# Second expert layer of each tile issued between the two halves of the next tile's first layer

## The chip, the cores and the metric

The kernel runs on one core of one Trainium2 chip. A core has five engines that run their own instruction streams and wait for each other by semaphores: TensorE (PE, matrix products, with its weight loads shown as PEld), VectorE (DVE), ScalarE (ACT), GpSimd (POOL) and SyncE (SP, which here only issues transfers). Each engine has a sequencer that reads its instructions in order and hands them on; the sequencer itself executes waits, branches, register arithmetic and loads of a register from memory. The metric is the device time of one launch in microseconds (us), lower is better. Before the change the median of three runs is 1127.79 us (1126.37 to 1128.49).

## The reference

1250 tokens of 1024 numbers in fp32. A two-layer graph convolution over 40,000 edges comes first, then a mixture of experts. The part that matters here is the second one:

```python
t = layernorm(x)                                   # 1250 x 1024
logits = silu(t @ rw1 + rb1) @ rw2 + rb2           # 8 experts
w = softmax over the 2 largest logits of each token, 0 elsewhere
eh = silu(einsum('td,edh->teh', t, ew1) + eb1)     # 1024 -> 256 hidden, per expert
eo = einsum('teh,ehd->ted', eh, ew2) + eb2         # 256 -> 1024, per expert
out = x + t + einsum('te,ted->td', w, eo)
```

Every token needs two of the eight experts only.

## The kernel before, in words

The graph layers and the router run first and are not touched. For the experts the kernel sorts the 2500 pairs of token and expert into tiles of 128 slots, each tile belonging to one expert, which is known only at run time. 23 tiles (0 to 22) are worked on in this execution. All expert weights lie in one on-chip buffer `xw`; which part a product reads is an address worked out from the tile's expert number, loaded into a register (`values_load`, L1511) by PE's and ACT's sequencers.

The steps of one tile, by the names of the code:

- `gather(i)` (L1492, POOL): an indirect DMA brings the tile's 128 token rows into one of three buffers.
- `spread_bias(i)` (L1487, SP): a DMA spreads the expert's output bias over 128 partitions into one of four buffers `ybs`.
- `fetch(i)` (L1503, L1506): eight PE transposes into PSUM and two ACT copies give the tokens transposed, `xT`.
- `first_layer(i)` (L1511, L1520, L1526): PE's and ACT's sequencers load the expert number; then eight matrix products of 128x128 by 128x256 accumulate in one PSUM buffer `ps`. Each is two instructions in the trace (fp32), so x16. A DVE copy (L1526; ACT for tile 0) takes the result into `hx`.
- `turn_hidden(i)` (L1533, L1535): two PE transposes of `hx` and two ACT activations (SiLU) give the hidden values transposed, `hT`.
- `second_layer(i)` (L1542, L1547, L1552, L1553): ACT scales the bias by the slot weight; four products (x8 in the trace) fill two PSUM buffers of 512 columns; two DVE instructions (L1552) weight the result and add the bias into `yo`, one of two buffers; POOL issues an indirect DMA that adds the 128 rows to the output (the scatter). All scatters add to the same tensor, so each waits until the one before it has landed.

`section` runs the tiles as a pipeline. In the step of tile i it issues, in this order: the gather for tile i + 3, the bias and `fetch` of tile i + 1, `turn_hidden` of tile i - 1, then `first_layer(i)` and `second_layer(i - 1)`. The order on PE and ACT is that of the code (a manual schedule); on DVE, POOL and SP a scheduler sets it when the program is built. `first_layer` takes an optional function `middle`, called between its fourth and fifth product. Tiles 1 and 3 use it for parts of the plan of the remaining tiles (`slots`, `slot_weights`), tile 0 too.

Tiles 0 to 19 always run. Behind them come branches on the number of tiles (`sections`, L1599): tiles 20 to 22 form the section that runs here, with tile 19's second half of the work joined to it. `end_of_last` then does `turn_hidden` and `second_layer` of tile 22 alone. In that section's last step (tile 22), where no `fetch` is due, `second_layer(21)` already stands in the middle of `first_layer(22)`: `early` is set there and nowhere else.

Of the kernel before, what the change touches and what calls it, by code (L numbers as in the profile page):

```python
# [29 lines left out]
def kernel(  # L30
# [967 lines left out]
    def moe():  # L998
# [383 lines left out]
        def slot_weights(at_tile, nb, i0, i1, take):  # L1382
            n = i1 - i0
            at_w = take([P, 2 * nb, 3, n], BF)
            at_w = at_w.rearrange("p (c b) i t -> p c b i t", c=2)
            for i in range(3):
                tt(
                    at_w[:, :, :, i, :], at_tile,
                    w_parts[i][:, :, :nb, None].to_broadcast([P, 2, nb, n]), ALU.mult,
                )  # L1390
            pw = by_slot(lambda c, b: at_w[:, c, b].rearrange("p i t -> p (i t)"), nb, 3 * n)
            nc.vector.tensor_reduce(
                w_slot[:, i0:i1], pw.rearrange("p (i t) -> p t i", t=n), AX.X, ALU.add
            )
# [87 lines left out]
        def spread_bias(i):  # L1482
            e = nc.values_load(
                eid[0:1, i : i + 1], engines=(ENG.SP,), min_val=0, max_val=E - 1,
                skip_runtime_bounds_check_because="eid is a count of experts, cut at E - 1",
            )
            nc.sync.dma_start(  # L1487
                out=ybs[i % 4], in_=eb2[ds(e, 1), :].partition_broadcast(P)
            )

        def gather(i):
            nc.gpsimd.indirect_dma_start(  # L1492
                out=xgs[i % 3], out_offset=None, in_=t_d[:N, :],
                in_offset=bass.IndirectOffsetOnAxis(ap=ids[:, i : i + 1], axis=0),
            )

        def fetch(i):
            xg = xgs[i % 3]
            xT = xTb[i % 2]
            for q in range(0, KD, 4):  # L1500
                pt = tpp.tile([P, 4, P], F32, name="tp")
                for k in range(4):
                    nc.tensor.transpose(  # L1503
                        pt[:, k, :], xg[:, (q + k) * P : (q + k + 1) * P], ident
                    )
                nc.scalar.copy(xT[:, q : q + 4, :], pt)  # L1506
            return xT

        def first_layer(i, xT, middle=None):

            e = nc.values_load(  # L1511
                eid[0:1, i : i + 1], engines=(ENG.PE, ENG.Activation),
                min_val=0, max_val=E - 1,
                skip_runtime_bounds_check_because="eid is a count of experts, cut at E - 1",
            )
            ps = mm.tile([P, 512], F32, name="ps")
            for k in range(KD):
                if k == KD // 2 and middle is not None:
                    middle()
                nc.tensor.matmul(  # L1520
                    ps[:, :H], xT[:, k, :], w1_all[:, ds(e, 1), k * H : (k + 1) * H],
                    start=(k == 0), stop=(k == KD - 1),
                )
            hx = hxs[i % 2]

            (nc.scalar.copy if i == 0 else nc.vector.tensor_copy)(hx, ps[:, :H])  # L1526
            return e, hx

        def turn_hidden(i, e, hx):
            pt = mm.tile([P, 512], F32, name="ps").rearrange("p (q n) -> p q n", n=P)  # L1530
            hT = hTs[i % 2]
            for q in range(KH):
                nc.tensor.transpose(pt[:, q, :], hx[:, q * P : (q + 1) * P], ident)  # L1533
            for q in range(KH):
                nc.scalar.activation(  # L1535
                    hT[:, q, :], pt[:, q, :], AF.Silu, bias=eb1_p[:, ds(e, 1), q : q + 1]
                )
            return e, hT

        def second_layer(i, e, hT):  # L1540
            yo, yb = yos[i % 2], ybs[i % 4]
            nc.scalar.activation(yb, yb, AF.Copy, scale=w_slot[:, i : i + 1])  # L1542
            for h in range(2):
                dc = slice(h * HALF, (h + 1) * HALF)
                ps = mm2.tile([P, 512], F32, name="ps2")
                for q in range(KH):
                    nc.tensor.matmul(  # L1547
                        ps, hT[:, q, :],
                        w2_all[:, ds(e, 1), q * D + h * HALF : q * D + (h + 1) * HALF],
                        start=(q == 0), stop=(q == KH - 1),  # L1550
                    )
                stt(yo[:, dc], ps, w_slot[:, i : i + 1], yb[:, dc], op0=ALU.mult, op1=ALU.add)  # L1552
            nc.gpsimd.indirect_dma_start(  # L1553
                out=out[:, :],
                out_offset=bass.IndirectOffsetOnAxis(ap=to[:, i : i + 1], axis=0),
                in_=yo, in_offset=None, bounds_check=N - 1, oob_is_err=False,
                compute_op=ALU.add,
            )
# [6 lines left out]
        xTs, held = {}, {}  # L1565

        def section(i0, i1, joined=True, until=None, middle=None):

            for i in range(i0, i1):
                if i + 3 < NTILE and i > 1:  # L1570
                    gather(i + 3)
                ahead = i + 1 < (until or i1)
                if ahead:
                    spread_bias(i + 1)
                    xTs[i + 1] = fetch(i + 1)
                rest = None
                if i > i0 or joined:
                    turned = turn_hidden(i - 1, *held.pop(i - 1))
                    rest = lambda: second_layer(i - 1, *turned)

                early = rest if not ahead and until is None else None
                held[i] = first_layer(i, xTs.pop(i), middle or early)
                if rest is not None and early is None:
                    rest()

        def sections(i0, ends):
            last = held.pop(i0 - 1)

            def end_of_last():
                second_layer(i0 - 1, *turn_hidden(i0 - 1, *last))  # L1590

            if not ends:
                end_of_last()
                return

            joined = i0 == always
            if not joined:
                end_of_last()
            with tc.If(n_tiles > i0) as more:  # L1599
                spread_bias(i0)  # L1600
                xTs[i0] = fetch(i0)
                if joined:
                    held[i0 - 1] = last
                section(i0, ends[0], joined)
                sections(ends[0], ends[1:])
            if joined:
                with more.Else():
                    end_of_last()
# [32 lines left out]
        with tc.manual_schedule(engines={ENG.PE, ENG.Activation}):  # L1641
            xTs[0] = fetch(0)
            xTs[1] = fetch(1)
            plan = plan_rest()
            next(plan)
            held[0] = first_layer(0, xTs.pop(0), lambda: next(plan))
            gather(3)
            at_b = []

            def slots():  # L1650
                at_b.append(next(plan))
                gather(4)

            section(1, 2, until=always, middle=slots)
            section(2, 3, until=always)
            n_tiles = nc.values_load(all_i[0:1, 0:1], min_val=0, max_val=NTILE)
            weights(NA_B, NB_B, sel_b, carver(SC[:, :512]))
            take_w = carver(scratch[:, 800:])
            section(
                3, 4, until=always,  # L1660
                middle=lambda: slot_weights(at_b[0], NB, NT_A, NTILE, take_w),
            )
            section(4, always, until=always)
            ok = nc.values_load(plain[0:1, 0:1], min_val=0, max_val=1)
            sections(always, ends)
# [43 lines left out]
```

## Time and profile before

| what | value |
| --- | --- |
| median of three runs | 1127.79 us |
| the profiled execution's own time | 1127.53 us |
| its span, first to last instruction | 1125.6 us |
| PE busy | 1089.8 us (97%) |
| expert tiles, from the first `first_layer` to the last scatter's issue | 924.18 to 1112.92 us |
| start of one `first_layer` to the next, tiles in mid-section | 7.98 us |
| scatter, from issue to landing (min, median, max) | 5.9, 6.6, 7.7 us |
| PE's register load L1511 (min, median, max of 23) | 306, 712, 1143 ns |
| ACT's register load L1511 (min, median, max of 23) | 273, 278, 467 ns |

A row of the timeline gives start and duration in us from the start of the span, engine, line, operation, what is written and read, the shape, how many instructions are merged into the row (x8), and in brackets how long the engine had been idle and what it waited for. Rows of one engine overlap a little, since matrix products are pipelined. A "q" behind an engine's name (PEldq, POOLq) means its sequencer.

### The profile page before, as it was taken

To read this page: it belongs to the slowest core of one execution; us is meant where nothing else is said; L and a number is where in the kernel's file an instruction comes from. 1 tells how busy PE (TensorE), PEld (TensorE's weight loads), DVE (VectorE), ACT (ScalarE), POOL (GpSimd) and SP (SyncE) were. 2 spreads that over 40 slices of the span, in tenths; PEclk is the share of its full clock that TensorE was granted. 3 is DMA by queue.
4 is the path that set the end of the run, shared out by engine and by line. 5 is a ranking of instruction groups with operands and counts; after the bars stand their busy time and mean duration, and the time that the engine had idled before them with its cause. 6 is when DMAs were issued, how large, how long until landed. Compare 5 with 4: busy or idle time off the path is not lost.

```text
span 1125.6 us, 13224 instructions
## 1 busy us (share of the span) xinstructions
PE 1089.8 (97%) x4729; PEld 786.4 (70%) x4729; DVE 467.7 (42%) x1145; ACT 188.0 (17%) x421; POOL 332.3 (30%) x438
## 2 busy tenths in 40 slices
PE   5999999999999999999999999999999999999994
PEld 4555556888888886888688868886544487676762
DVE  8767777762121236333134223364522173222221
ACT  5300001001111111110011000022211124232321
POOL 1899999900000000003002202254000013232321
PEclk9999999999999999999999999999999999999997
DMA  7111011010100021032103270244870456767762
GB/s 231 38 38 14 27 38 38 1 38 1 38 1 1 1 75 37 1 116 97 45 1 131 92 270 4 81 163 169 305 246 1 149 186 167 195 175 192 193 170 48
DMA packets 62317, 107.33 MB, mean 95 GB/s; under 512 B 8906, under 2 KB 35690, under 8 KB 62240
## 3 DMA queue, kind: packets, MB, share of 16 engines
q1 hardware_dynamic: 51392, 79.69, 20.8%
q0 software_dynamic: 7056, 23.88, 9.0%
q10 hardware_dynamic: 3792, 2.79, 0.8%
q8 instruction: 42, 0.69, 0.3%
q14 instruction: 35, 0.29, 0.1%
HBM read 80.74 MB, written 27.42 MB: 96 GB/s over the span
## 4 chain that ended last, share of the span: by engine, by line
PE 79%; DMA 12%; issue 3%; DVE 2%; ACT 2%; POOL 1%; POOLq 0%; ACTq 0%; DVEq 0%
PE ps L515 12%; DMA out_dram<-L 12%; PE ps L449 11%; PE psb L629 10%; PE ps L699 8%; PE ps L551 8%; PE ps L629 7%; PE ps L1175 5%; PE ps L616 5%; PE ps L1189 4%; PE cnt L410 3%; PE ps L1128 2%; POOL ol L400 1%; PE tp L309 1%; DVE L L140 1%
## 5 line engine op out<-in xcount | busy, mean ns | idle before, releaser
L400 POOL TENSOR_SCALAR ol<-lane,keys 125x128 f16<-125x128 f16 x320 | 193.3, 623 | 28.0 <-DVE oh L407 28.0
L449 PE MATMUL ps<-h0T,L 128*128 128x498 f32 (+2 forms) x384 | 147.0, 515 | 0.2 <-ACT h0T L312 0.2
L695 POOL TENSOR_TENSOR L<-L 128x512 f32<-128x512 f32 (+1 forms) x20 | 32.1, 1614 | 374.8 <-DMA L<-in_L_gnn_b_dram 216.3
L515 PE MATMUL ps<-L,h0T 128*128 128x256 f32 (+1 forms) x640 | 141.9, 379 | 0.0
L515 PEld LDWEIGHTS ps<-L,h0T 128*128 128x128 f32 (+1 forms) x640 | 118.4, 187 | 17.7 <-issue 0.2
L407 DVE TENSOR_SCALAR oh<-win,keys 125x240 f16<-125x240 f16 x320 | 85.1, 322 | 32.9 <-PE cnt L410 31.2
L449 PEld LDWEIGHTS ps<-h0T,L 128*128 128x128 f32 x384 | 67.1, 190 | 38.1 <-issue 33.4
L1520 PE MATMUL ps<-xw,L 128*128 x368 | 84.1, 380 | 0.7 <-issue 0.7
L1547 PE MATMUL ps<-xw,L 128*128 x184 | 82.8, 593 | 0.5 <-ACT L L1535 0.5
L551 PE MATMUL ps<-C,yh 128*128 128x256 f32 (+2 forms) x240 | 81.8, 356 | 0.0
L551 PE MATMUL ps<-C,yl 128*128 128x256 f32 (+2 forms) x240 | 81.5, 353 | 0.0
L699 PE MATMUL ps<-zh,C 128*128 128x512 f32 (+1 forms) x200 | 79.5, 398 | 0.0
L699 PE MATMUL ps<-zl,C 128*128 128x512 f32 (+1 forms) x200 | 78.6, 393 | 0.0
L1520 PEld LDWEIGHTS ps<-xw,L 128*128 128x128 f32 x368 | 68.0, 190 | 9.5 <-issue 1.4
L1553 POOL DMA_INDIRECT out_dram<-L x23 | 36.5, 1587 | 118.2 <-DVE L L1552 91.4
L429 DVE TENSOR_TENSOR C<-C,cnt 128x240 f32 x160 | 64.4, 402 | 12.4 <-DVE C L429 0.8
L1492 POOL DMA_INDIRECT L<-t_d,L x26 | 25.5, 982 | 143.9 <-DVE L L140 123.1
L1547 PEld LDWEIGHTS ps<-xw,L 128*128 128x128 f32 x184 | 34.9, 190 | 34.9 <-issue 32.3
L410 PEld LDWEIGHTS <-ol 125*128 125x128 f16 x320 | 31.0, 97 | 37.3 <-POOL ol L400 21.7
L1552 DVE SCALAR_TENSOR_TENSOR L<-ps,L 128x512 f32<-128x512 f32 x46 | 34.5, 751 | 53.1 <-PE ps L1547 53.1
L381 DVE TENSOR_TENSOR yl<-ps,yh 128x256 fp32r<-128x256 f32 (+1 forms) x40 | 17.0, 424 | 92.4 <-ACT yh L380 92.4
L140 DVE TENSOR_TENSOR L<-L,ps 128x512 f32<-128x512 f32 (+1 forms) x28 | 17.1, 611 | 86.7 <-PE ps L1175 44.5
(222 smaller groups left out, 1524.0 us busy)
## 6 DMA issues: line engine op xcount, KB each, us to landing
xw<-in_L_ffn_ew_dram SPq DMA_DIRECT2D x16, 1024.0 KB, 10.6
L<-in_L_ffn_eb_dram SPq DMA_DIRECT2D x23, 512.0 KB, 4.1
L<-in_x_dram SPq DMA_DIRECT2D x20, 256.0 KB, 2.8
v_d<-L SPq DMA_DIRECT2D x18, 256.0 KB, 2.0
xa<-v_d SPq DMA_DIRECT2D x18, 256.0 KB, 5.8
t_d<-L SPq DMA_DIRECT2D x9, 512.0 KB, 4.3
out_dram<-xa SPq DMA_DIRECT2D x9, 512.0 KB, 2.7
L<-in_L_gnn_W_self_dram SPq DMA_DIRECT2D x4, 1024.0 KB, 5.7
```

What stands on the lines that cost most here:

```text
L400: nc.gpsimd.tensor_scalar(ol[:, c, :], lane[:GP], keys[:, 1, c, r : r + 1], None, op0=ALU.is_equal)
L407: nc.vector.tensor_scalar(oh, win[:GP], keys[:, 0, i * GC + c, r : r + 1], None, op0=ALU.is_equal)
L410: nc.tensor.matmul(ps[:, i, :GW], ol[:, i * GC + c, :], oh, start=(c == 0), stop=(c == GC - 1),)
L429: nc.vector.tensor_tensor(to, to.bitcast(F32), ps[:, i, :GW].rearrange("p (k w) -> p k w", k=NB), ALU.add,)
L449: nc.tensor.matmul(ps[:, :n], w[:, k, (d % 2) * P : (d % 2 + 1) * P], h0T[:, k, c0 : c0 + n], start=(k == 0), stop=(k == KD - 1),)
L515: nc.tensor.matmul(ps[:m, :QW], hT[:, k, blk(b)], w[:, k, :], start=(k == 0), stop=(k == KD - 1))
L551: nc.tensor.matmul(ps[:, :n], part[: rows[k], k, (d % 2) * P : (d % 2 + 1) * P], C[: rows[k], k, c0 : c0 + n], start=(k == 0 and part is y ...
L616: nc.tensor.matmul(ps[:m], hT1[:, k, blk(b)], w[:, k, :], start=(k == 0), stop=(k == KD - 1))
L629: nc.tensor.matmul(ps, rows_of(k), w[:, k, :], start=(first and k == 0), stop=(k == KB - 1), skip_group_check=not first,)
L699: nc.tensor.matmul(ps[:m], C[: rows[k], k, blk(b)], part[: rows[k], k, :], start=(k == 0 and part is yh), stop=(k == NB - 1 and part is yl),)
L1520: nc.tensor.matmul(ps[:, :H], xT[:, k, :], w1_all[:, ds(e, 1), k * H : (k + 1) * H], start=(k == 0), stop=(k == KD - 1),)
L1547: nc.tensor.matmul(ps, hT[:, q, :], w2_all[:, ds(e, 1), q * D + h * HALF : q * D + (h + 1) * HALF], start=(q == 0), stop=(q == KH - 1),)
```

## The change

In `section`, the second layer of tile i - 1 is handed to `first_layer(i)` as `middle` in every step where `middle` is not taken already; before, this was so only in the last step of a branch's section. Which instructions are issued, and how many, is the same. On PE the four products of the second layer move ahead of the last four products of the first layer, in the steps of tiles 2 and 4 to 21; the step of tile 22 had this order already, and the steps of tiles 1 and 3 keep theirs. The orders on ACT, POOL and SP stay as they were. On DVE the two L1552 instructions of tile i - 1 move ahead of the L1526 copy of tile i.

```diff
@@ section @@
                     turned = turn_hidden(i - 1, *held.pop(i - 1))
                     rest = lambda: second_layer(i - 1, *turned)
 
-                early = rest if not ahead and until is None else None
-                held[i] = first_layer(i, xTs.pop(i), middle or early)
-                if rest is not None and early is None:
+                held[i] = first_layer(i, xTs.pop(i), middle or rest)
+                if rest is not None and middle is not None:
                     rest()
```

The DVE order in the step of tile 2, where the plan's last work also runs on DVE, is (by lines, before and after):

```
before: L140, L1526(2), L1371 ... L1323, L1378, L140, L140, L1552(1), L1378, L140, L140, L1552(1), L1378, L140
after:  L140, L1552(1), L1371 ... L1323, L1552(1), L1378, L140, L140, L1378, L140, L140, L1526(2), L1378, L140
```

## The prediction

> **What bounds the kernel now.** I read the page first, then the timeline of a tile in mid-section, then the waits at the tile borders, and the end of the chain last.
>
> ```profile
> PE 1089.8 (97%) x4729; PEld 786.4 (70%) x4729; DVE 467.7 (42%) x1145; ACT 188.0 (17%) x421; POOL 332.3 (30%) x438
> ```
>
> PE is full. The expert part is no exception: in a mid-section step PE's rows meet end to start, and the next step starts 7.98 us later.
>
> ```profile
> 1005.63 3.60 PE L1547 MATMUL ps<-xw,L 128*128 x8
> 1005.83 0.42 DVE L1526 COPY L<-ps 128x256 f32<-128x256 f32 x1 [3.80 <-PE ps L1520]
> 1009.06 1.04 PE L1503 MATMUL tp<-ident,L 128*128 128x128 f32 x8
> 1009.26 0.75 DVE L1552 SCALAR_TENSOR_TENSOR L<-ps,L 128x512 f32<-128x512 f32 x1 [0.91 <-PE ps L1547]
> 1009.94 0.38 PE L1533 MATMUL ps<-ident,L 128*128 128x128 f32 x2
> 1010.15 3.62 PE L1520 MATMUL ps<-xw,L 128*128 x16
> 1010.29 1.59 POOL L1553 DMA_INDIRECT out_dram<-L  x1 [5.11 <-DVE L L1552]
> ```
>
> The DVE copy of the hidden values ends at 1006.25; the transposes L1533 that need it come at 1009.94. So 3.7 us of cover, given by the second layer. After 1009.06 + 0.95 the second L1552 is done, and the scatter leaves 0.28 later.
>
> What PE's sequencer does shows in its register load L1511, which stands behind L1533 in the program: in this step it runs at 1006.31, 0.06 behind the end of the copy, with L1533 not due for 3.6 us. So the sequencer stops at L1533's wait, goes on once the copy is done, and loads the expert number ahead of time. That load is not short:
>
> ```profile
> L1511 PEldq TENSOR_LOAD <-L x23: 306/712/1143, 923.3 to 1094.6; - x23
> L1511 PEldq TENSOR_LOAD <-L x1: 801/801/801, 1006.3 to 1006.3; - x1
> L1511 PEldq TENSOR_LOAD <-L x1: 306/306/306, 928.4 to 928.4; - x1
> ```
>
> One place of the old kernel already has the order that the change makes everywhere: tile 0, whose first layer is followed at once by the next fetch, with the copy on ACT instead of DVE.
>
> ```profile
> 927.71 1.04 PE L1503 MATMUL tp<-ident,L 128*128 128x128 f32 x8
> 927.96 0.37 ACT L1526 COPY L<-ps 128x256 f32<-128x256 f32 x1 [4.34 <-PE ps L1520]
> 928.58 0.38 PE L1533 MATMUL ps<-ident,L 128*128 128x128 f32 x2
> 928.90 1.99 PE L1520 MATMUL ps<-xw,L 128*128 x8
> 930.72 0.66 PE L1346 MATMUL tp<-L 128*128 128x23 f16 x20
> ```
>
> The copy ends at 928.33, the load runs 928.38 to 928.69, an address calculation follows, and the first product starts at 928.90.
>
> The end, from the chain of work that ended last: the last scatter waits for the landing of the one before, not for its data (ready at 1110.60).
>
> ```profile
> 1105.49 6.67 DMA out_dram<-L
> 1112.93 1.54 POOL out_dram L1553
> ```
>
> **The change part by part.** It removes and adds no instruction; the work of PE is the same.
>
> *Earlier scatters.* Four products (8 x 0.215 = 1.72 us, from 1097.58 to 1099.31 in the step that has the order already) now stand behind the second layer, so L1552, the scatter, and SP's next bias load, which waits for the same L1552, come 1.72 us earlier. In mid-section nobody waits for them. At the end the gain has a ceiling: tile 22's data are ready at 1110.60 + 0.28 = 1110.88 and the scatter left at 1112.92, so at most 2.04 us. POOL keeps its order (gather, scatter, gather), and both move together; ACT keeps its order too. The split of the accumulation costs nothing: in the step of tile 22 the halves take 1.73 us each and no gap stands between.
>
> *Second layer's wait for SiLU.* It now has half a first layer of cover. In mid-section the activations end 2.30 us behind the start of the fetch (at 1011.36 of 1009.06); the second layer would start at 1.09 + 1.73 = 2.82. Hidden, with 0.5 us left; the cover gone would cost that difference per tile.
>
> *Wait for the hidden copy, and the register load behind it.* The copy moves from the start of the second layer to the start of the fetch. It ends 0.62 us in (0.20 + 0.42); the fetch lasts 0.88, so the transposes themselves are still covered. What is late next is the register load: it starts at 0.67, and the first product stands 0.57 behind the copy's end, at 1.19 instead of 1.09. Tile 0's row shows all of it: 930.72 - 927.71 = 3.01 us for fetch, turn and half a first layer, against 0.88 + 0.21 + 1.73 = 2.82. So 0.19 us per tile. The lower bound is 0 (the lead suffices), the upper 0.59 (a load of 0.71, the median, in place of 0.31). I take 0.19, because the long loads run while the scatter's packets fill all DMA engines, whereas the load now comes 1.46 us behind the second L1552, while the bias load runs; another register load of PE under a bias load took
>
> ```profile
> L1656 PEldq TENSOR_LOAD <-L x1: 310/310/310, 939.1 to 939.1; - x1
> ```
>
> It applies where a step of the new order is followed by a fetch: tiles 4 to 18 and tile 20, 16 times: 3.0 us. Tile 19 is followed by the branch and by a wait of the second fetch for ACT (1081.29), which hide it.
>
> *Tile 2.* Its copy now stands in DVE's queue behind two L1552 and two groups of the plan's work. Before, DVE worked without a gap from 941.37 until the third group began at 946.02; without the copy's 0.33 that is 945.6, and the copy ends at about 946.0. The first product follows 0.57 later, at 946.6 instead of 945.55, plus the 0.09 that the second product lost in tile 0's row: 1.1 us. Bounds: 0 (if DVE's order lets the copy through sooner) and 1.4 (a load of 0.6). The second layer of tile 1 loses nothing by the queue: its L1552 waits for PE only.
>
> *Tile 21.* No fetch follows, so nothing covers the copy. Tile 22, alone at the end, shows this already:
>
> ```profile
> 1105.15 0.44 PE L1533 MATMUL ps<-ident,L 128*128 128x128 f32 x2 [0.52 <-DVE L L1526]
> ```
>
> The transposes stand 0.68 behind the end of the products (1102.74 + 1.73). The first product comes at 1.19 instead of 0.22, plus 0.09: 1.06 us.
>
> *Sum.* PE ends 1.1 + 3.0 + 1.06 = 5.2 us later; tile 22's data could leave at 1116.1. Scatter 21 leaves with its data, at 1103.69 + 0.28 + 5.2 = 1109.2 (scatter 20, 1.72 earlier and 4.1 later, has landed by then), and 22 follows 6.9 to 7.4 behind it (1098.59 to 1105.49, 1105.49 to 1112.92): 1116.1 to 1116.6, against 1112.92. That is +3.5 us; what lies behind (12.7 us to the end of the span) stays. The profiled execution took 1127.53, so 1131.0; the median lies 0.26 above it: 1131.3.
>
> A rule on the load: the Trainium skill, "DMA: Bandwidth & Descriptors", Latency and other measured facts, gives a tensor_load a floor of about 0.6 us. This trace has 0.306 on PE and 0.273 on ACT, so the measurement decides. By the page the load would be 0.29 longer 18 times, and the estimate some 1136.5.
>
> **The rivals.**
>
> *All is hidden (not slower).* If PE's sequencer has enough queued work at each tile, only the earlier scatters count. For it: PE shows no gap in 20 tiles, and the cover that is left misses by only 0.1 us. Against: tile 0's row. The time: scatter 20 leaves 1.72 earlier and the end follows, 1.7 us, up to the ceiling of 2.04: 1126.1. It decides if the copy's end plus 0.57 is below 1.09.
>
> A rule that would favour this: "TensorE: Matmul & The Clock Gate" (its table, engine queue depth) has PE's queue 64 deep with weight loads pulled ahead. The trace has the sequencer stopped at the wait for the copy all the same, at 1006.31.
>
> *Only the two exposed places cost.* Tile 2 and tile 21 lose 2.2 us, the others nothing. Data 22 at 1113.1, scatter 21 at 1106.2 and 22 at 1113.1 to 1113.6: +0.5, so 1128.3.
>
> *The load is slow here too.* If the bias load or a scatter that comes in its way stretches it to the median of 0.71, each tile loses 0.59: 16 x 0.59 + 2.2 + 0.8 = 12.4, less the 2.04 that the end had in hand: 10.4, so 1138. At 0.49 (the load at 923.3) it is 0.37 a tile: 16 x 0.37 + 2.2 + 0.4 - 1.7 = 6.8, so 1134.6.
>
> **How the numbers follow.** My forecast 0.62, only two places 0.12, all hidden 0.12, slow load 0.14. 0.2% is 2.3 us, about what a measurement of this kernel can tell from no change. The forecast's own range, 1129.5 to 1134, gives slower 0.57 and same 0.05; two places is same; hidden is same 0.08 and faster 0.04, since its ceiling is 0.18%; slow load is slower. Together faster 0.04, same 0.25, slower 0.71. The range of 1128.0 to 1135.5 leaves out the hidden case and the worst loads.
>
> **What would show it.** In the profile after: PE's L1511 some 0.67 behind the start of L1503 and about 0.3 long; rows of PE from L1503 to the next L1503 of 8.17 instead of 7.98; a gap ahead of L1533 of about 0.5 in the step of tile 22, and one of 0.7 at 945.3 in the step of tile 3; DVE's L1526 ending at about 946. Wrong it would be with steps of 7.98 (hidden), of 8.4 or more (slow load), or with PE waiting at L1547 for ACT.

## The result and the profile after

| | before | after |
| --- | --- | --- |
| median of six runs, us | 1127.36 (1126.37 to 1128.49) | 1132.32 (1131.80 to 1134.35) |
| ratio of the times | | 1.0041, 95% interval 1.0029 to 1.0052 |
| first `turn_hidden` of PE (L1533, tile 0) to the last, us | 176.57 | 183.55 |
| first `turn_hidden` to the last scatter's issue, us | 184.34 | 189.28 |
| PE's register load L1511, min / median / max, ns | 306 / 712 / 1143 | 297 / 303 / 972 |

The kernel is slower, by 4.96 us of 1127. The profiled execution of the changed kernel took 1134.35 us, 2.0 above its median; 1.70 of that was there before, since the first `turn_hidden` stands at 930.28 instead of 928.58: in this execution the granted clock of PE was 0.94 on the mean from 900 to 928 us, and 1.00 in the profile before, and 0.06 of 28 us is 1.7. From 928 us on it is 1.00 in both. So the two traces are compared from that instruction on, and there the last scatter leaves 189.28 - 184.34 = 4.94 us later, nearly the 4.96 between the medians.

The page hardly shows it. PE's share is 97% in both kernels. Its busy time has grown by 6.4 us, from 1089.8, with the same 4729 instructions: small gaps count as busy, since the ends of matrix products are modelled and a row's end can reach over the gap behind it.

```profile
PE 1096.2 (97%) x4729; PEld 787.8 (70%) x4729; DVE 467.3 (41%) x1145; ACT 187.8 (17%) x421; POOL 331.2 (29%) x438
```

The timeline of one tile in mid-section does show it (start, duration, engine, line):

```profile
1021.40 1.04 PE L1503 MATMUL tp<-ident,L 128*128 128x128 f32 x8
1021.60 0.42 DVE L1526 COPY L<-ps 128x256 f32<-128x256 f32 x1 [0.97 <-PE ps L1520]
1022.27 0.38 PE L1533 MATMUL ps<-ident,L 128*128 128x128 f32 x2
1022.60 1.99 PE L1520 MATMUL ps<-xw,L 128*128 x8
1023.05 0.64 ACT L1535 ACTIVATE L<-ps,eb_p 128x128 f32<-128x128 f32 x2
1024.42 3.60 PE L1547 MATMUL ps<-xw,L 128*128 x8
1027.86 1.89 PE L1520 MATMUL ps<-xw,L 128*128 x8
1028.06 0.75 DVE L1552 SCALAR_TENSOR_TENSOR L<-ps,L 128x512 f32<-128x512 f32 x1 [0.91 <-PE ps L1547]
1029.09 1.59 POOL L1553 DMA_INDIRECT out_dram<-L  x1 [5.32 <-DVE L L1552]
1029.58 1.04 PE L1503 MATMUL tp<-ident,L 128*128 128x128 f32 x8
```

Look at three distances. From fetch to fetch (1021.40 to 1029.58) it is 8.18 us instead of 7.98. From the fetch to the first product (1021.40 to 1022.60) it is 1.20 instead of 1.09. From `turn_hidden` to that product (1022.27 to 1022.60) it is 0.33, where the old kernel had 0.21. So 0.11 of the 0.20 are lost ahead of the first product; the other 0.09 lie in the first half of the layer, which lasts 1.82 (1022.60 to 1024.42) where the prediction's row had 1.73. What fills the gap is on no engine's row, but on the row of PE's sequencer: the register load, which starts 0.67 behind the fetch, as soon as the copy at 1021.60 has ended. The first row below is all 23 loads of PE, the second the one of this step, the third the one in the step of tile 20:

```profile
L1511 PEldq TENSOR_LOAD <-L x23: 297/303/972, 923.3 to 1105.6; - x23
L1511 PEldq TENSOR_LOAD <-L x1: 317/317/317, 1022.1 to 1022.1; - x1
L1511 PEldq TENSOR_LOAD <-L x1: 972/972/972, 1088.6 to 1088.6; - x1
```

The load itself has become shorter than in the old kernel (median 303 instead of 712 ns), and yet it costs time now and in mid-section cost none then. There it started 3.8 us ahead of the first product that needs it (1006.31 against 1010.15).

The rest is at single places. PE's waits from 936 us on (total us, times, longest) name them: four full stops at `turn_hidden` for the copy, where the old kernel had the last one only.

```profile
PE ps L1533 <- DVE L L1526: 2.1, 4, 0.5
PE ps L1547 <- ACT L L1535: 0.5, 1, 0.5
PE ps L1520 <- issue: 0.3, 1, 0.3
```

In the timeline these are tiles 2, 18, 21 and 22, and the 0.32 at 1089.80 is the long register load of 0.97 us:

```profile
947.26 0.42 DVE L1526 COPY L<-ps 128x256 f32<-128x256 f32 x1
947.73 0.44 PE L1533 MATMUL ps<-ident,L 128*128 128x128 f32 x2 [0.53 <-DVE L L1526]
...
1078.88 0.42 DVE L1526 COPY L<-ps 128x256 f32<-128x256 f32 x1 [0.97 <-PE ps L1520]
1079.36 0.44 PE L1533 MATMUL ps<-ident,L 128*128 128x128 f32 x2 [0.52 <-DVE L L1526]
...
1089.10 0.38 PE L1533 MATMUL ps<-ident,L 128*128 128x128 f32 x2
1089.80 1.99 PE L1520 MATMUL ps<-xw,L 128*128 x8 [0.32 <-issue]
...
1105.65 0.44 PE L1533 MATMUL ps<-ident,L 128*128 128x128 f32 x2 [0.52 <-DVE L L1526]
```

The end has changed its kind. The last scatter now follows its data. In the chain of work that ended last, POOL's wait for the landing of the scatter before (1118.67) is over by 1118.72, and 0.61 us pass behind it; the timeline, below the chain, shows that the second `L1552` ends at 1119.28 and the scatter follows it by 0.28:

```profile
1112.65 6.02 DMA out_dram<-L
...
1118.72 0.61 issue
...
1119.56 1.55 POOL out_dram L1553
```

```profile
1118.53 0.75 DVE L1552 SCALAR_TENSOR_TENSOR L<-ps,L 128x512 f32<-128x512 f32 x1 [0.91 <-PE ps L1547]
1119.56 1.55 POOL L1553 DMA_INDIRECT out_dram<-L  x1 [5.34 <-DVEq L1598]
```

### The profile page after: what moved, and what is told of

The parts are those of the page before. It is cut to its first block, busy times and chain, and to the rows that moved or that the text cites. A ratio compares the mean times of both kernels' runs of the same rounds, so it can differ in the third digit from the quotient of the medians.

```text
span 1132.4 us, 13224 instructions
## 1 busy us (share of the span) xinstructions
PE 1096.2 (97%) x4729; PEld 787.8 (70%) x4729; DVE 467.3 (41%) x1145; ACT 187.8 (17%) x421; POOL 331.2 (29%) x438
## 4 chain that ended last, share of the span: by engine, by line
PE 91%; DMA 2%; DVE 2%; ACT 2%; issue 1%; POOL 1%; ACTq 0%; POOLq 0%; DVEq 0%
PE ps L515 12%; PE ps L449 11%; PE psb L629 9%; PE ps L699 8%; PE ps L551 8%; PE ps L629 7%; PE ps L1520 6%; PE ps L1547 5%; PE ps L1175 5%; PE ps L616 5%; PE ps L1189 4%; PE cnt L410 3%; PE ps L1128 2%; DMA out_dram<-L 2%; PE tp L1503 1%
## 5 line engine op out<-in xcount | busy, mean ns | idle before, releaser
L1520 PE MATMUL ps<-xw,L 128*128 x368 | 90.7, 391 | 1.3 <-issue 1.0
L1547 PE MATMUL ps<-xw,L 128*128 x184 | 82.8, 593 | 0.5 <-ACT L L1535 0.5
L1552 DVE SCALAR_TENSOR_TENSOR L<-ps,L 128x512 f32<-128x512 f32 x46 | 34.5, 751 | 110.2 <-PE ps L1547 110.2
L1547 PEld LDWEIGHTS ps<-xw,L 128*128 128x128 f32 x184 | 34.9, 190 | 34.9 <-issue 29.4
L410 PE MATMUL cnt<-oh,ol 125*128 125x240 f16 x320 | 50.6, 265 | 2.7 <-POOL ol L400 2.1
```

What stands on the lines that cost most here:

```text
L410: nc.tensor.matmul(ps[:, i, :GW], ol[:, i * GC + c, :], oh, start=(c == 0), stop=(c == GC - 1),)
L1520: nc.tensor.matmul(ps[:, :H], xT[:, k, :], w1_all[:, ds(e, 1), k * H : (k + 1) * H], start=(k == 0), stop=(k == KD - 1),)
L1547: nc.tensor.matmul(ps, hT[:, q, :], w2_all[:, ds(e, 1), q * D + h * HALF : q * D + (h + 1) * HALF], start=(q == 0), stop=(q == KH - 1),)
```

## The experiments

The question was which of three things makes a step longer: the register load that stands behind the wait, the split of the first layer's accumulation, or the longer way of the SiLU. The theory was the load. An edit told as one in the changed order starts from the kernel after, the others from the kernel before.

### The register load ahead of the wait

In the changed order, the load of the expert number is moved ahead of `turn_hidden`, PE's and ACT's alike. The number is known long before; only its place in the program changes.

```diff
-        def first_layer(i, xT, middle=None):
-            e = nc.values_load(...)
+        def expert_of(i):
+            return nc.values_load(...)
+        def first_layer(i, xT, middle=None, e=None):
+            if e is None:
+                e = expert_of(i)
...
+                e = expert_of(i)
                 if i > i0 or joined:
                     turned = turn_hidden(i - 1, *held.pop(i - 1))
                     rest = lambda: second_layer(i - 1, *turned)
-                held[i] = first_layer(i, xTs.pop(i), middle or rest)
+                held[i] = first_layer(i, xTs.pop(i), middle or rest, e)
```

> The changed order, but the load of the expert number (PE's and ACT's) stands ahead of turn_hidden, so that PE's sequencer does it before it stops at the wait for the hidden copy. Theory (the register load behind that wait is what the steps pay): mid-section steps go from 8.18 back to 7.98 us; the copy itself stays exposed where nothing covers it, about 0.7 us each for tiles 2, 18 and 21, 2.2 us of PE in all, of which the end absorbs most: 0.2 to 0.7 us slower than before the change, ratio 1.000 to 1.001. Rival (splitting the first layer, or the earlier output traffic, costs PE 0.2 us a step): steps stay at 8.18 and the ratio at about 1.004.

Measured: 1127.35 us (12 runs) against 1127.73 before (29 runs), ratio 0.9997 (0.9988 to 1.0005). The timeline of this kernel (its copy is L1530, `turn_hidden` L1537, the first layer L1524):

```profile
1008.76 1.04 PE L1503 MATMUL tp<-ident,L 128*128 128x128 f32 x8
...
1016.74 1.04 PE L1503 MATMUL tp<-ident,L 128*128 128x128 f32 x8
1016.94 0.42 DVE L1530 COPY L<-ps 128x256 f32<-128x256 f32 x1 [0.97 <-PE ps L1524]
1017.61 0.38 PE L1537 MATMUL ps<-ident,L 128*128 128x128 f32 x2
1017.83 1.46 PE L1524 MATMUL ps<-xw,L 128*128 x6
```

and PE's register load, whose place in the program is now behind the fetch at 1008.76 and ahead of that step's `turn_hidden`:

```profile
L1510 PEldq TENSOR_LOAD <-L x1: 300/300/300, 1006.2 to 1006.2; - x1
```

The step is back at 7.98 (1008.76 to 1016.74), the first product at 1.09 behind the fetch (1016.74 to 1017.83), and the load starts 2.6 us ahead of its fetch. The copy still comes as late as in the changed order, the first layer is still split and the SiLU still has half a first layer of cover. So in mid-section the load behind the wait is the whole cost; the other two cost nothing. This edit moves ACT's load too; the next one touches PE's alone.

What is left against before is 1.34 us of PE's time: 0.68 each at tiles 18 and 21, where no fetch stands between the copy and `turn_hidden`, three losses of 0.06, and a gain of 0.20 at tile 0, whose load stood uncovered in the old kernel too. Tile 2 lost no more than one of the 0.06, unlike in the forecast: with the load in another place the scheduler put tile 2's copy earlier into DVE's order, and it ended at 944.91 instead of about 946. The 1.34 us fit into the 2.04 that the end had in hand, so the last scatter comes 183.64 behind the first `turn_hidden`, 0.70 sooner than before. The interval of the times reaches from a gain of 0.12% to a loss of 0.05%, so the expected loss of 0.2 to 0.7 us can't be told from no change.

### The register load twice

In the changed order, a second load of the same number by PE stands behind the first, and the last four products use it. If the load is the cost, doubling it must cost as much again.

```diff
+            e2 = nc.values_load(eid[32:33, i : i + 1], engines=(ENG.PE,), ...)
...
-                    ps[:, :H], xT[:, k, :], w1_all[:, ds(e, 1), ...],
+                    ps[:, :H], xT[:, k, :], w1_all[:, ds(e if k < KD // 2 else e2, 1), ...],
```

> The changed order with a second register load on PE, of the same number from another partition, right behind the first; the last four products of the first layer use it. Theory: each uncovered load costs its length and a gap of 0.1, about 0.4 us in some 18 steps, so mid-section steps of 8.58 and 7 us more than the change: 12 us slower than before, ratio about 1.0105. Rival (the load is not on the path): as the change, 1.004.

Measured: 1142.28 us (4 runs) against 1127.73 (29 runs), ratio 1.0126 (1.0109 to 1.0143). Its timeline (`turn_hidden` is L1538):

```profile
1016.69 1.04 PE L1503 MATMUL tp<-ident,L 128*128 128x128 f32 x8
...
1017.56 0.38 PE L1538 MATMUL ps<-ident,L 128*128 128x128 f32 x2
1018.27 1.99 PE L1524 MATMUL ps<-xw,L 128*128 x8 [0.33 <-issue]
...
1025.26 1.04 PE L1503 MATMUL tp<-ident,L 128*128 128x128 f32 x8
```

and the two loads of that step, one behind the other:

```profile
L1511 PEldq TENSOR_LOAD <-L x1: 301/301/301, 1017.4 to 1017.4; - x1
L1516 PEldq TENSOR_LOAD <-L x1: 297/297/297, 1017.8 to 1017.8; - x1
```

A step takes 8.57 here (8.58 and 8.59 in others), 0.40 more than after, and the way from `turn_hidden` to the first product is 0.71 instead of 0.33: the 0.30 of the load and about 0.1 around it. That is twice the 0.20 of the first load, part of which the fetch still covers; nothing is left to cover the second. The total is higher than expected in part because the second load is uncovered at 20 places behind the first `turn_hidden`, where some 18 were counted. At 0.40 each these are 8 us, and by the first `turn_hidden` to the last scatter's issue this kernel's profile is 197.09 - 189.28 = 7.8 us above that of after. The medians lie 10.0 apart; the 2 us more lie ahead of that instruction or in the spread of only four runs (1140.67 to 1144.31), and which of the two was not separated.

### The changed order in mid-section alone

```diff
-                early = rest if not ahead and until is None else None
+                early = rest if (not ahead and until is None) or 4 <= i <= 17 else None
```

> The old order with the new one in the steps of tiles 4 to 17 alone, each of them followed by a fetch. Theory: 14 times 0.20 us of PE, nothing gained at the end since scatter 20 is as late as PE: 2.8 us slower, ratio 1.0025. Rival (the cost lies at the two section ends and in tile 2 alone): within 0.3 us of before, ratio 1.000.

Measured: 1131.09 us (12 runs) against 1127.73, ratio 1.0035 (1.0024 to 1.0047). Two steps of its timeline, 8.17 and 8.20 us long:

```profile
1010.93 1.04 PE L1503 MATMUL tp<-ident,L 128*128 128x128 f32 x8
...
1019.10 1.04 PE L1503 MATMUL tp<-ident,L 128*128 128x128 f32 x8
...
1027.30 1.04 PE L1503 MATMUL tp<-ident,L 128*128 128x128 f32 x8
```

PE's time to the last `turn_hidden` grows by 179.55 - 176.57 = 2.98 us over 14 steps: eleven at 0.19 to 0.21, two at 0.23 and one at 0.35. The last scatter is 3.04 later. Here none of it is absorbed, since the steps at the end keep the old order and the last scatter still waits for the landing of the one before. So the many small losses alone carry more than half of the slowdown.

### The changed order in the steps of tiles 2, 19 and 21 alone

```diff
-                early = rest if not ahead and until is None else None
+                early = rest if (not ahead and until is None) or i in (2, 19, 21) else None
```

> The old order with the new one in the steps of tiles 2, 19 and 21 alone, that is where the copy of tile 2 falls behind DVE's plan work, and where no fetch covers turn_hidden of tiles 18 and 21 (19 stands for 18: its step ends the first section; the rest of the steps keep the old order). Theory: tile 2 1.1, tile 21 1.25, and at the first section's end little, since tile 19's copy is covered by the branch and the double fetch: 2.3 to 2.9 us of PE, of which the earlier scatter 20 gives 1.7 back: 0.6 to 1.3 us slower, ratio 1.0005 to 1.0012. Rival (the middle steps cost nothing, all of the loss is here): 5 us slower, 1.004.

Measured: 1127.91 us (12 runs) against 1127.73, ratio 1.0007 (0.9995 to 1.0019). Its timeline at tile 2, at tile 21 and at the last scatter:

```profile
945.80 0.44 PE L1533 MATMUL ps<-ident,L 128*128 128x128 f32 x2 [0.54 <-DVE L L1526]
...
1098.90 0.44 PE L1533 MATMUL ps<-ident,L 128*128 128x128 f32 x2 [0.52 <-DVE L L1526]
...
1112.80 1.55 POOL L1553 DMA_INDIRECT out_dram<-L  x1 [5.34 <-DVEq L1599]
```

PE loses 2.16 us, 1.08 at tile 2, 1.06 at tile 21, nothing at tile 19. But the last scatter comes only 0.12 later, 184.46 instead of 184.34 behind the first `turn_hidden`: the second layer of tile 20, brought early in the step of tile 21, lets the scatters at the end leave sooner and gives back the 2.04 us for which the last one had been held up by a landing. So the exposed places and the gain at the end nearly cancel, as the sum of the prediction had it.

### The early second layer where it pays, with cover

Only the end gains from an early second layer. So this kernel keeps the old order, loads the number ahead, gives the new order to the step of tile 21 alone, and moves the last fetch (of tile 22) behind the first layer of tile 21, where it covers the copy.

```diff
                 ahead = i + 1 < (until or i1)
+                late = until is None and i == i1 - 2
                 if ahead:
                     spread_bias(i + 1)
-                    xTs[i + 1] = fetch(i + 1)
+                    if not late:
+                        xTs[i + 1] = fetch(i + 1)
                 rest = None
+                e = expert_of(i)
...
-                early = rest if not ahead and until is None else None
-                held[i] = first_layer(i, xTs.pop(i), middle or early)
+                early = rest if until is None and i >= i1 - 2 else None
+                held[i] = first_layer(i, xTs.pop(i), middle or early, e)
+                if late:
+                    xTs[i + 1] = fetch(i + 1)
```

> The old order, the register load ahead of turn_hidden, and the new order only in the step of tile 21, whose fetch (tile 22) moves behind first_layer(21), so that it covers the copy there. Theory: tile 20's second layer ends 2.6 us earlier (1.72 by its place, 0.88 by the fetch), scatter 20 then leaves with the landing of 19, about 1.3 us earlier; PE loses about 0.3 us where tile 22's first product waits for ACT's copies; the last scatter leaves about 1.2 us earlier and the ratio is about 0.999. Rival (the end is not bound by the chain of scatters): 1.000 or above.

Measured: 1126.16 us (11 runs) against 1128.20 before (23 runs), ratio 0.9985 (0.9976 to 0.9994): faster than the kernel before by 0.15%, and by more than the kernel after, which was 0.41% slower than it. Its timeline at tile 21 (copy L1530, `turn_hidden` L1537):

```profile
1096.53 1.04 PE L1503 MATMUL tp<-ident,L 128*128 128x128 f32 x8
1096.73 0.42 DVE L1530 COPY L<-ps 128x256 f32<-128x256 f32 x1 [0.97 <-PE ps L1524]
1097.40 0.38 PE L1537 MATMUL ps<-ident,L 128*128 128x128 f32 x2
1097.86 1.99 PE L1524 MATMUL ps<-xw,L 128*128 x8
```

and its chain of work that ended last:

```profile
1090.65 6.06 DMA out_dram<-L
...
1097.52 5.89 DMA out_dram<-L
...
1104.35 6.21 DMA out_dram<-L
...
1111.33 1.54 POOL out_dram L1557
```

The copy lies under the fetch, and PE loses 0.34 us there instead of 1.06, which with the 0.20 that the early load gains at tile 0 leaves 0.15 in all. The last scatter leaves 182.51 behind the first `turn_hidden`, 1.83 sooner than before. That is nearly all that could be had: 2.04 less 0.15 is 1.89, and the second weighting of tile 22 (L1556 here) ends at 1110.98, 0.34 ahead of the scatter. The 2.04 is the figure of one execution, in which the landing before the last scatter took 6.67 us.

### The early load in the old order

The kernel before, with the register load ahead of `turn_hidden` and nothing else, as a control for the kernel above:

```diff
+                e = expert_of(i)
                 if i > i0 or joined:
...
-                held[i] = first_layer(i, xTs.pop(i), middle or early)
+                held[i] = first_layer(i, xTs.pop(i), middle or early, e)
```

> The old order with the register load ahead of turn_hidden, nothing else: a control for the two kernels with that load. Theory: the load was hidden already where the second layer covers the copy, so the time is that of before, ratio 1.000. Rival (an early load gains by itself): below 0.998.

Measured: 1128.00 us (12 runs) against 1128.20, ratio 0.9998 (0.9990 to 1.0007): nothing. PE's wait for the copy is the single one that before had, too.

```profile
PE ps L1537 <- DVE L L1530: 0.5, 1, 0.5
```

So the gain of the kernel with the covered end does not come from the early load. In the old order that load is covered in either place, but for tile 0, where it stood uncovered before. There the first product now follows 0.22 behind `turn_hidden` instead of 0.32, and the step is 0.20 us shorter, as the theory has it:

```profile
928.40 0.38 PE L1537 MATMUL ps<-ident,L 128*128 128x128 f32 x2
928.62 1.89 PE L1524 MATMUL ps<-xw,L 128*128 x8
```

The end does not follow, since the last scatter waits for the landing of the one before (7.30 us in this profile): it leaves 184.60 behind the first `turn_hidden`.

## Why the prediction was right, and where its sum was not

The mechanism held: a register load behind a late wait, at nearly every tile. The two experiments on the load, moved away and doubled, show it, and the steps below say what each term measured. That the time came so near, 1132.32 us for a forecast of 1131.3, is in part luck: the slowdown was 4.96 us where 3.5 was forecast, and the median of six runs before lies 0.43 below that of the three from which the forecast started.

**Earlier scatters.** Right. The end gave back 2.04 us, all that it had in hand; the prediction counted 1.5 to 2.0, since it let the last scatter follow 6.9 to 7.4 behind the one before. It followed at 6.91, with its data.

**Second layer's wait for SiLU.** Right: PE's list of waits has L1547 waiting for ACT once, which is the last tile alone at the end.

**Wait for the hidden copy, 0.19 a tile.** Right in size and in its parts: load 0.67 behind the fetch, 0.30 to 0.32 long, first product 0.11 late, step 8.17 to 8.22 in 12 of the 13 steps that start with tiles 4 to 16, and 8.33 in one. In that one (and in the same step of the kernel with the new order in mid-section alone) the first product comes later behind a load of 0.30, and no row shows why. They sum to 2.81 us where 13 x 0.19 = 2.47 was counted.

**Tile 2, 1.1.** Right: 1.08. The copy ended at 945.98 on the clock of before (947.68 - 1.70), where about 946.0 was forecast.

**Tile 21, 1.06.** Right: 1.06.

**Tile 18, counted at 0.19 among the sixteen.** Wrong: 1.07. The prediction put it that the 0.19 "applies where a step of the new order is followed by a fetch: tiles 4 to 18 and tile 20". Tile 18 is followed by none. `section` for tiles up to 19 ends its own pipeline there, so in the step of tile 19 `ahead` is false, and the fetch of tile 20 stands behind the branch. The copy is as uncovered as that of tile 21, and the row at 1079.36 is the twin of the one at 1105.65. This was to be read from the code, not from the profile.

**Tile 19, counted at nothing.** Wrong: 0.58. The branch and the wait of the second fetch were to hide it, and would have hidden a load of 0.3. The load at 1088.62 took 0.97, and the first product came 0.70 behind `turn_hidden` instead of 0.22; the products behind it lost the other 0.10. This is the rival of the slow load, at a single place. In the kernel with the changed order in three steps alone, tile 19 lost nothing.

Together PE lost 6.98 us instead of 5.2, and with 2.04 absorbed the end moved by 4.94 where 3.5 was forecast. The difference of 1.8 in PE's time is tile 18 (0.88), tile 19 (0.58) and the sum of the small steps (0.34).

**The rivals.** "All is hidden" was refuted by steps of 8.18. "Only the two exposed places" was run as a kernel of its own and gave 1.0007 (0.9995 to 1.0019), where the prediction had worked out 0.5 us, 1.0004. "The load is slow here too" held at one tile.

**The two rules.** The Trainium skill, "DMA: Bandwidth & Descriptors", Latency and other measured facts, puts a tensor_load at no less than about 0.6 us. The loads of PE after the change have a minimum of 297 and a median of 303 ns, so the measurement decides against the page here. "TensorE: Matmul & The Clock Gate" (its table, engine queue depth) gives PE a queue of 64 instructions, with weight loads pulled ahead of running products. No row of these traces contradicts the depth, but the steps of 8.18 show that it did not carry PE over a wait of 0.6 us and a register load of 0.3 behind it.

## What to carry to other kernels

When a wait is moved later on an engine that reads its instructions in order, count not only the datum waited for but every sequencer instruction behind the wait up to the next product: here 0.3 us of register load cost 0.20 us at each tile in mid-section, and moving it one place ahead of the wait took all of that away. Check for each step, also at the ends of sections and at branches, that the work which covers the wait stands there at all. An earlier result pays only where somebody waits for it: in mid-section it was worth nothing, at the end up to 2.04 us, and the version that moved it there alone, with its cover, was the only one with a gain clear of the noise: 0.15%, with an interval of 0.06% to 0.24%.

## What the runs showed of the hardware

The prediction took the long register loads of PE for a matter of full DMA engines: short under a bias load, long under a scatter's packets. The first half holds, the second only in part. What tells the lengths apart best is how long ago POOL issued a scatter. In the eight traces the 81 loads less than 1.6 us behind a scatter's issue took 0.30 to 0.32 us, and the 31 loads more than 4.2 us behind it 0.30 to 0.31. Of the 84 loads in between, all 2.0 to 4.2 us behind it, 80 took 0.44 to 1.61 us, one 0.37 and three 0.31 (one each before, with the load ahead and with three steps alone, all at 982 to 983 us). The very first load stands outside this: at 923.3, ahead of all scatters, it took 0.49 us in the kernel before. That the DMA engines are full does not settle it: they were busy 0.96 of the time during the load of 317 ns at 1022.1, under a bias load, and 0.96 during one of 297 ns at 1054.08, 4.3 behind a scatter, in the changed order with the load ahead; during the one of 801 ns at 1006.31 it was 1.01. In these last two only packets of the queue of POOL's transfers ran. In the kernel before, behind the scatter at 1002.31, that queue moves nothing in the first 2 us and fills 0.74 of the engines' time in the next 2, so the long loads begin about when its packets do, and end while they still run.

Examples: in the kernel before, the load of 801 ns at 1006.31 stands 4.0 behind the scatter at 1002.31. After the change the load of 317 ns at 1022.1 stands 1.2 behind the scatter at 1020.90, and the one of 972 ns at 1088.62 stands 2.3 behind the scatter at 1086.35. In the old order with the early load most loads fall into the long phase:

```profile
L1510 PEldq TENSOR_LOAD <-L x23: 297/1192/1614, 923.1 to 1091.6; - x23
```

There they cost nothing, since they are covered: that kernel's steps in mid-section are still 7.98 us long. ACT's loads of the same number keep a median of 278 ns in the kernels before and after, and 0.47 us at most. A gather's issue follows 1.9 us behind each scatter's in mid-section, so the two hardly stand apart; but a load 1.1 us behind a second gather's issue and 4.3 behind the scatter's (at 1085.2, the gather at 1084.08, the scatter at 1080.89, in the old order with the early load) took 305 ns. No run separates the scatter's packets from whatever else stands at that distance, and why PE's load and not ACT's should be the one that stretches stays open.

Also not expected: the place of a register load changed DVE's order. In the kernel with the changed order and the load ahead, the scheduler put the first `L1552` of tile 1 before the plan's work and tile 2's copy before a part of it that it had stood behind, and the 1.08 us of that tile were gone but for 0.06. How much of that is the order's and how much the load's was not separated; at tiles 18 and 21 the load was 0.38 of the 1.06, and if it is as much here (an estimate), the order gave 0.7.
